# A planner that draws moved ranks stretch by stretch instead of for the whole order

## The chip, the cores and the metric

The kernel runs on one core of a Trainium2 chip. The time is that of one launch on the device in microseconds; it is the median of several runs. A profile of one further execution gives the busy time of each engine: TensorE (PE, with its weight loads as PEld), VectorE (DVE), ScalarE (ACT), GpSimd (POOL), and SyncE (SP), which issues the DMA transfers.

## The reference

One decoder layer over x of 32 sequences x 256 tokens x 256 features, all in float32. Three blocks follow each other, each on a layer norm of x and each added to x:

```python
x = x + self_attention(layernorm(x))   # gated slot attention, 4 heads, 64 slots
x = x + cross_attention(layernorm(x))  # 16 heads of 16, over 77 context rows, masked
x = x + experts(layernorm(x))          # 8 experts of rank 64, two of them weighted per token
```

The self attention projects to q, k (4 x 32), v (4 x 64), slot scores s (4 x 64) and a gate g. q, k and v go through a causal convolution of four taps and a SiLU, q and k through a rotation. Then come two causal linear attentions: q against k with the slot weights as values (`ok`), a softmax over the slots, and that against the slots with v as values (`ov`); in both, the weights are exp(s) over their running sum. A norm per head, the gate and an output projection end it. The cross attention is a plain softmax attention. The experts' hidden part is silu(u) * v for all eight experts, weighted by a softmax over the two largest router logits, and multiplied by the output weights.

## The kernel before

Everything works on one sequence at a time (the experts on two, 512 tokens; the last two sequences singly). The kernel's Python holds a planner, and the order in which instructions are issued to the engines is the planner's. Every engine then runs its own instructions in that order, and semaphores make one wait for the data or the buffer of another.

**Threads.** The work of a sequence is written as generators: `self_attention(n)`, `cross_attention(n)`, `experts(n, count)` and the parts that they start (`queries_keys`, `value`, `slot_weights`, `output_gate`, `weigh`, `context`, `weights`, `chunk`, `spread_weights`). At each step a generator yields what it wants: an engine and a time in ns, a list of alternatives, a buffer (`Take`), or an event. `ATTENTIONS` = 5 chains of self attentions, `CROSSINGS` = 3 chains of cross attentions and 2 chains of experts run at the same time; a further chain, `loads`, issues the loads of weights and of x on SyncE's queue.

**The clock of the plan.** `Flow.run` is a list scheduler over the planner's own cost figures. It takes, again and again, the step that can begin first, and among those that could begin at the same time the one of the lowest rank, since `threads` is sorted by rank:

```python
key = begin, whole, not thread[7]
if best is None or key < best[0]:
    best = key, wish, thread
```

Where a step offers alternatives, the one that ends first is taken. So `copy` goes to ScalarE or VectorE, `combine` (L647) to VectorE or GpSimd, `product` to VectorE or to ScalarE and GpSimd, and a convolution tap (L824) to VectorE or to ScalarE and GpSimd (L828, L831), as each engine is free in the plan. A changed order therefore also changes how much work each engine gets. PSUM is four single banks and two double ones, given out by `bank`; buffers in SBUF come in fixed numbers (`shapes`).

**Ranks.** `Flow.rank` gives a stage's start plus the sequence number plus a moved amount:

```python
return stage + n + self.moved.get((stage, n), 0.0)
```

with stages 0.0 (self attention), -1.0 (cross attention) and 3.0 (experts). A small move can put one sequence's steps behind or ahead of another's where both could begin.

**The search for moves.** `best_order` runs the whole plan on stand-ins (`Sketch`) 70 times. Each time it takes the best moves so far, redraws 20 of the 96 keys from a normal distribution with deviation 0.3, and keeps the result if the planned end is not later. The plan with the kept moves then emits the instructions.

**Names on TensorE.** In the order of a sequence's life: hT_ps (transposed layer norm, L680), s_ps, g_ps (L725), pr_ps (q, k and v, L716), ET_ps, v_ps (transposes, L880 for v), cp_ps<-qk, ok_ps<-cp (L739, L782), ok_ps and WT_ps (transposes), cp_ps<-WT, ov_ps (L739, L782), o_ps, oT_ps (transposes), wo_ps. Cross attention: K_ps, V_ps (L1127), hT_ps, Q_ps, sc_ps (L1183), eT_ps (L1241), av_ps (L1260), pj_ps. Experts: hT_ps, lgT_ps (L1304), lg_ps (L1312), wt_ps (L1362), u_ps and ev_ps (L716), eo_ps (L1461, and L1484 with wB_ps for the last two). cp_ps, ok_ps<-cp, ov_ps, sc_ps, av_ps and lgT_ps use only some rows or columns of the array and are issued in packed groups. On VectorE the heavy steps of self attention are the taps (L824), the causal masks (L758, L768), the running sums and reciprocals (L912, L918), and the statistics of the layer norm (L690, L691).

Of the kernel before, what the change touches and what calls it, by code (L numbers as in the profile page):

```python
# [43 lines left out]
PE, DVE, ACT, POOL, SP = "PE", "DVE", "ACT", "POOL", "SP"  # L44
# [6 lines left out]
RANK_SELF, RANK_CROSS, RANK_EXPERTS = 0.0, -1.0, 3.0  # L51
# [39 lines left out]

ORDERS, MOVED, BY = 70, 20, 0.3


class Sketch:


    def __init__(self, shape=(1,)):  # L100
        self.shape = tuple(shape)
# [53 lines left out]
class Flow:  # L155
# [6 lines left out]

    def __init__(self, slots, moved=None):
        self.moved = moved or {}
        self.slots = {tag: [(0.0, i) for i in range(n)] for tag, n in slots.items()}


        self.parts = WHOLE
        self.banks = {"bank": [0.0] * slots["bank"], "bank2": [0.0] * slots["bank2"]}
        self.free = defaultdict(float)  # L170

        self.port = 0.0
        self.busy = defaultdict(float)
        self.threads = []
        self.finish = 0.0
        self.count = 0

        self.changed = False

    def start(self, rank, part):  # L180
        self.count += 1
        thread = [rank, self.count, self.finish, part, None, None, 0.0, 0]
        thread[4] = next(part)
        self.threads.append(thread)
        self.threads.sort(key=lambda t: t[:2])
        self.changed = True

    def rank(self, stage, n):
        return stage + n + self.moved.get((stage, n), 0.0)

    def event(self):
# [86 lines left out]
    def run(self):  # L278
        while True:
            self.settle()  # L280
            if not self.threads:
                return
            best = None
            for thread in self.threads:
                wish = thread[4]
                if isinstance(wish, list):

                    _, begin, wish = min(self.end(thread, w) for w in wish)
                elif isinstance(wish, tuple):
                    begin = self.begin(thread, wish[0])  # L290
                else:
                    continue
                whole = False
                if wish[0] == PE:
                    _, _, tag, parts = wish
                    whole = parts is WHOLE
                    if tag:
                        got = self.bank(tag)
                        if not got:
                            continue  # L300
                        begin = max(begin, got[0] + HOP[PE])
# [5 lines that stand above are left out]
            if not best:  # L307
                raise Stuck
            (begin, _, _), wish, thread = best
            if wish[0] == PE and wish[3] != self.parts:  # L310
                begin = max(begin, self.free[PE] + SWITCH)
            engine, ns = REAL[wish[0]], wish[1]
            self.free[engine] = begin + ns
            if wish[0] in (BOTH, PAIR):
                self.port = begin + ns
            self.busy[engine] += ns
            thread[2] = begin + ns + TAIL.get(engine, 0.0)
            thread[5], thread[6] = engine, begin + ns
            if engine == SP:
                landing = Event()  # L320
                landing.time = begin + ns + LANDING
                self.resume(thread, landing)
            elif engine == PE:
                _, _, tag, self.parts = wish
                got = None
                if tag:
                    _, kind, slot = self.bank(tag, hold=True)
                    slots = slot if tag == "quad" else [slot]
                    got = [Buffer(self, kind, i, 1) for i in slots]
                    for buf in got:  # L330
                        buf.owner = thread
                    thread[7] += len(got)
                    got = got if tag == "quad" else got[0]
                self.resume(thread, got)
            else:
                self.resume(thread, wish[:2])


def best_order(plan, slots, sequences):


    rng = random.Random(0)
    keys = [
        (stage, n)
        for stage in (RANK_SELF, RANK_CROSS, RANK_EXPERTS) for n in range(sequences)
    ]
    best, kept = None, {}
    for _ in range(ORDERS):
        moved = dict(kept)
        if best is not None:  # L350
            moved.update({key: rng.gauss(0, BY) for key in rng.sample(keys, MOVED)})
        flow = Flow(slots, moved)
        try:
            plan(flow)
        except Stuck:
            continue
        if best is None or flow.finish <= best:
            best, kept = flow.finish, moved
    return kept


@with_exitstack
def decoder_layer(
# [28 lines left out]
    B, T, D = x.shape  # L392
# [29 lines left out]
    slots = {tag: s[0] for tag, s in shapes.items() if isinstance(s, tuple)}  # L422

    def lay_out(flow, nc, const, work, small, dram, psum):
# [363 lines left out]
        def self_attention(n):  # L788
# [58 lines left out]
            def queries_keys():  # L847
                yield have["k"]
                y2 = yield from conv_silu2(((wq_s, 0), (wk_s, 0)), (0, 1), "cv_qk")
                yield have["table"]  # L850
                y2.uses = 2

                yr = yield from take("rp")
                yield DVE, dve(512)
                nc.vector.stream_shuffle(yr.tile, y2.tile, SWAP)
                y2.drop()
                qk = yield from take("qk")
                yield from combine(qk.tile, y2.tile, cos.unsqueeze(1).to_broadcast(FEA), ALU.mult)
                y2.drop()
                yield from combine(yr.tile, yr.tile, sin.unsqueeze(1).to_broadcast(FEA), ALU.mult)  # L860
                yield from combine(qk.tile, qk.tile, yr.tile, ALU.add)
                yr.drop()
                got = yield from causal_products(qk.tile[:, 1:2, :], qk.tile[:, 0:1, :], HK)
                qk.drop()

                def weigh(c):
                    prods[c] = yield from causal_weights(got[c])
                    flow.set(ready[c])

                flow.start(rank, weigh(1))  # L870
                yield from weigh(0)
# [647 lines left out]
            flow.start(0, all_experts(i))  # L1519
        flow.run()  # L1520

    moved = best_order(lambda flow: lay_out(flow, *[Sketch()] * 6), slots, B)
    with tc.manual_schedule():
        lay_out(Flow(slots, moved), nc, const, work, small, dram, psum)

# [61 lines left out]
```

## Time and profile before

| what | us |
|---|---|
| median of 3 runs (1366.28 to 1367.6) | 1367.16 |
| the profiled execution | 1367.22 |
| its span, first to last instruction | 1365.4 |
| TensorE busy | 1316.1 (96%) |
| TensorE weight loads busy | 971.0 (71%) |
| VectorE busy | 1145.0 (84%) |
| ScalarE busy | 1040.9 (76%) |
| GpSimd busy | 634.2 (46%) |
| mean granted TensorE clock | 0.989 of full |

In the profile, the rows of digits cut the span into 40 slices of 34 us and give the busy share of each in tenths; PEclk is the clock that TensorE was granted. A row of a stretch gives the length, then the busy time of each engine with its number of instructions. A line of waits names who waited for whom, the total, how often, and the longest. Matmuls overlap, and the ends in the trace are modelled, so TensorE can be busy and yet not run at its best rate.

### The profile page before, as it was taken

To read this page: it belongs to the slowest core of one execution; us is meant where nothing else is said; L and a number is where in the kernel's file an instruction comes from. 1 tells how busy PE (TensorE), PEld (TensorE's weight loads), DVE (VectorE), ACT (ScalarE), POOL (GpSimd) and SP (SyncE) were. 2 spreads that over 40 slices of the span, in tenths; PEclk is the share of its full clock that TensorE was granted. 3 is DMA by queue.
4 is the path that set the end of the run, shared out by engine and by line. 5 is a ranking of instruction groups with operands and counts; after the bars stand their busy time and mean duration, and the time that the engine had idled before them with its cause. 6 is when DMAs were issued, how large, how long until landed. Compare 5 with 4: busy or idle time off the path is not lost.

```text
span 1365.4 us, 27161 instructions
## 1 busy us (share of the span) xinstructions
PE 1316.1 (96%) x9345; PEld 971.0 (71%) x9345; DVE 1145.0 (84%) x2268; ACT 1040.9 (76%) x4160; POOL 634.2 (46%) x805
## 2 busy tenths in 40 slices
PE   6989989999999999999999999999999999999898
PEld 5767766676868776876778678678676876757665
DVE  6999999777887976998789889998988799966554
ACT  4668898867878876886888678788888786886741
POOL 1546654524465724347543555554444355534220
PEclk9899999999999999999999999999999999999999
DMA  4600010122111122111121120111111211021110
GB/s 129 139 2 2 13 19 4 30 63 64 42 40 44 27 58 55 49 29 32 48 51 39 34 48 3 42 35 19 33 43 48 64 29 34 17 60 45 43 40 24
DMA packets 134202, 55.91 MB, mean 41 GB/s; under 512 B 106168, under 2 KB 125880, under 8 KB 134064
## 3 DMA queue, kind: packets, MB, share of 16 engines
q1 hardware_dynamic: 134064, 54.17, 16.7%
q8 instruction: 74, 1.21, 0.4%
q14 instruction: 64, 0.52, 0.1%
HBM read 42.37 MB, written 11.79 MB: 40 GB/s over the span
## 4 chain that ended last, share of the span: by engine, by line
PE 67%; DVE 25%; ACT 5%; POOL 2%; issue 1%; DMA 0%; ACTq 0%; DVEq 0%; POOLq 0%
PE ev_ps L716 8%; PE u_ps L716 8%; PE eo_ps L1461 6%; DVE y L824 5%; PE cp_ps L739 4%; PE eT_ps L1241 3%; PE av_ps L1260 3%; DVE RzT L918 3%; PE pj_ps L725 3%; PE pr_ps L716 3%; PE wo_ps L725 3%; PE sc_ps L1183 3%; PE ov_ps L782 3%; PE Q_ps L716 3%; PE hT_ps L680 2%; PE s_ps L725 2%
## 5 line engine op out<-in xcount | busy, mean ns | idle before, releaser
L1211 ACT ACTIVATE s<-s,s_mx 128x77 f32<-128x77 f32 x1024 | 359.0, 356 | 38.3 <-DVE s_mx L1206 38.0
L1211 ACT ACTIVATION_READ_ACCUMULATOR s<-s,s_mx 128x1 f32 x1024 | 201.5, 197 | 0.0
L824 DVE SCALAR_TENSOR_TENSOR y<-pr_ps,conv,y 128x254 f32<-128x254 f32 (+2 forms) x368 | 149.1, 469 | 4.7 <-ACT y L811 4.5
L671 POOL TENSOR_TENSOR rs_r<-rs_r,mhalf 128x2 f32<-128x2 f32 (+1 forms) x128 | 128.1, 1001 | 10.7
L702 ACT ACTIVATE ln_h<-xs,ln_off,rs_r 128x256 f32<-128x256 f32 x192 | 110.8, 597 | 22.8 <-POOL ln_off L696 21.3
L1191 DVE TENSOR_TENSOR s<-sc_ps,cap 128x616 f32<-128x616 f32 x128 | 98.7, 784 | 26.9 <-PE sc_ps L1183 26.7
L716 PE MATMUL ev_ps<-hT_e,ev_s 128*128 128x512 f32 (+1 forms) x272 | 120.8, 572 | 0.1
L716 PE MATMUL u_ps<-hT_e,eu_s 128*128 128x512 f32 (+1 forms) x272 | 119.1, 571 | 0.4 <-DVE y L824 0.4
L647 POOL TENSOR_TENSOR esT<-e_th,wB 128x512 f32<-128x512 f32 x55 | 73.3, 1335 | 93.0 <-DVE e_th L1415 74.1
L1461 PE MATMUL eo_ps<-eo_s,esT 128*128 128x256 f32 x480 | 115.6, 384 | 0.0
L670 POOL TENSOR_SCALAR rs_r<-ln_mv 128x2 f32<-128x2 f32 x96 | 25.6, 267 | 185.6 <-DVE ln_mv L691 167.2
L918 DVE RECIPROCAL RzT<-RzT 128x256 f32<-128x256 f32 x64 | 110.7, 1733 | 0.0
L1461 PEld LDWEIGHTS eo_ps<-eo_s,esT 128*128 128x128 f32 x480 | 87.4, 190 | 14.0 <-issue 3.3
L968 ACT ACTIVATE ok<-ok,ok_mx 128x64 f32<-128x64 f32 x256 | 87.4, 344 | 8.9 <-DVE ok_mx L965 8.9
L1241 PE MATMUL eT_ps<-cst,s 128*128 128x128 f32 x640 | 88.3, 278 | 3.8 <-POOL s L647 1.7
L1206 DVE TENSOR_REDUCE s_mx<-s 128x16 f32<-128x1232 f32 x64 | 91.1, 1423 | 0.8
L1241 PEld LDWEIGHTS eT_ps<-cst,s 128*128 128x128 f32 x640 | 75.6, 143 | 18.4 <-issue 7.0
L647 POOL TENSOR_TENSOR s<-s,s_rs 128x1232 f32<-128x1232 f32 x28 | 63.2, 2257 | 53.7 <-DVE s_rs L1217 53.6
L690 DVE BATCH_NORM_STATS2 ln_st<-xs 128x6 f32<-128x256 f32 x192 | 78.4, 408 | 8.0 <-DMA xs<-in_x_dram 7.6
L716 PEld LDWEIGHTS u_ps<-hT_e,eu_s 128*128 128x128 f32 x272 | 49.3, 190 | 42.3 <-issue 39.0
L758 DVE TENSOR_TENSOR cp<-cp_ps,cst 128x768 f32<-128x768 f32 x78 | 72.5, 939 | 6.1 <-PE cp_ps L739 6.1
L638 ACT ACTIVATE eT<-eT_ps 128x1024 f32<-128x1024 f32 x64 | 65.6, 1026 | 14.6 <-PE eT_ps L1241 14.4
(167 smaller groups left out, 3432.5 us busy)
## 6 DMA issues: line engine op xcount, KB each, us to landing
wB<-wd SPq DMA_DIRECT2D x60, 256.0 KB
Vb<-spread_v SPq DMA_DIRECT2D x32, 320.0 KB
xs<-in_x_dram SPq DMA_DIRECT2D x32, 256.0 KB
out_dram<-xs SPq DMA_DIRECT2D x32, 256.0 KB
cx<-in_ctx_dram SPq DMA_DIRECT2D x32, 77.0 KB
spread_v<-V SPq DMA_DIRECT2D x32, 77.0 KB
spread_v<-zeros SPq DMA_DIRECT2D x2, 309.0 KB
mk<-in_mask_Bx1xSxS_bk_dram SPq DMA_DIRECT2D x32, 19.2 KB
```

The lines of the kernel that those rows point to most:

```text
L647: engines[engine].tensor_tensor(to, a, b, op)
L671: nc.gpsimd.tensor_tensor(r, r, mhalf[:, :n], ALU.pow)
L702: nc.scalar.activation(h.tile[:, t, :], xt[:, t, :], AF.Identity, bias=off[:, t : t + 1], scale=rstd[:, t : t + 1],)
L716: nc.tensor.matmul(ps, lhsT=w[:, d], rhs=hT[:, d, :], start=(d == 0), stop=(d == ND - 1))
L725: nc.tensor.matmul(pv[:, t, :], lhsT=hT[:, d, ts(t, P)], rhs=w[:, d, :], start=(d == 0), stop=(d == n - 1),)
L824: nc.vector.scalar_tensor_tensor(y.tile[:, u, s:], now, by, y.tile[:, u, s:], ALU.mult, ALU.add)
L918: nc.vector.reciprocal(Rz.tile[:, c, :], Rz.tile[:, c, :])
L1191: nc.vector.tensor_tensor(sv[:, 2 * a : 2 * a + 2], got[a].tile[:, :, : ND * QR * S2].rearrange("p r (h k) -> p r h k", k=S2), cap.tile[:, ...
L1206: nc.vector.tensor_reduce(mx.rearrange("p (q h) -> p q h", h=QH), sv, AX.X, ALU.max, negate=True)
L1211: nc.scalar.activation(sv[:, h // QH, h % QH, :], sv[:, h // QH, h % QH, :], AF.Exp, bias=mx[:, h : h + 1], accum_out=sm[:, h : h + 1],)
L1241: nc.tensor.transpose(flat[:, ts(NTT * i + t, P)], s[t].tile[:, column : column + P], ident)
L1461: nc.tensor.matmul(halves(ps.tile)[:, t, :], lhsT=sT.tile[:, d, ts(NTT * b + t, P)], rhs=eo_s[:, d, :], start=(d == 0), stop=(d == NEC - 1),)
```

## The change

`best_order` no longer judges whole plans. It goes through the plan in stretches of 200 us of planned time. For each, it plans from the beginning to 50 us past the stretch with the moves kept so far, and then 16 times with new moves for about half of those keys whose rank had not been asked for before the stretch began. It keeps the moves with which TensorE has had most work planned by that point. When a plan reaches its end, the planned end decides. `Flow` notes when each rank is asked for (`asked`) and stops planning at `until`. The planner's costs, the generators and the instructions themselves are as before.

```diff
--- before.py
+++ after.py
@@ -91,7 +91,8 @@
 
 
 
-ORDERS, MOVED, BY = 70, 20, 0.3
+
+DRAWS, STRETCH, BEYOND, MOVED, BY = 16, 200000.0, 50000.0, 0.5, 0.3
 
 
 class Sketch:
@@ -162,6 +163,8 @@
 
     def __init__(self, slots, moved=None):
         self.moved = moved or {}
+
+        self.asked, self.until = {}, math.inf
         self.slots = {tag: [(0.0, i) for i in range(n)] for tag, n in slots.items()}
 
 
@@ -186,6 +189,7 @@
         self.changed = True
 
     def rank(self, stage, n):
+        self.asked[stage, n] = self.finish
         return stage + n + self.moved.get((stage, n), 0.0)
 
     def event(self):
@@ -307,6 +311,8 @@
             if not best:
                 raise Stuck
             (begin, _, _), wish, thread = best
+            if begin > self.until:
+                return
             if wish[0] == PE and wish[3] != self.parts:
                 begin = max(begin, self.free[PE] + SWITCH)
             engine, ns = REAL[wish[0]], wish[1]
@@ -336,27 +342,39 @@
                 self.resume(thread, wish[:2])
 
 
-def best_order(plan, slots, sequences):
+def best_order(plan, slots):
 
 
     rng = random.Random(0)
-    keys = [
-        (stage, n)
-        for stage in (RANK_SELF, RANK_CROSS, RANK_EXPERTS) for n in range(sequences)
-    ]
-    best, kept = None, {}
-    for _ in range(ORDERS):
-        moved = dict(kept)
-        if best is not None:
-            moved.update({key: rng.gauss(0, BY) for key in rng.sample(keys, MOVED)})
+
+    def drawn(moved, until):
         flow = Flow(slots, moved)
+        flow.until = until
         try:
             plan(flow)
         except Stuck:
-            continue
-        if best is None or flow.finish <= best:
-            best, kept = flow.finish, moved
-    return kept
+            return -math.inf, flow
+        if flow.threads:
+            return flow.busy[PE] - max(0.0, flow.free[PE] - until), flow
+
+        return 1e9 - flow.finish, flow
+
+    kept, begin = {}, 0.0
+    while True:
+        until = begin + STRETCH + BEYOND
+        best, flow = drawn(kept, until)
+        free = [key for key, at in flow.asked.items() if at >= begin]
+        choice = kept
+        for _ in range(DRAWS):
+            moved = dict(kept)
+            moved.update({key: rng.gauss(0, BY) for key in free if rng.random() < MOVED})
+            done, other = drawn(moved, until)
+            if done > best:
+                best, choice = done, moved
+        kept = choice
+        begin += STRETCH
+        if best > 0.5e9:
+            return kept
 
 
 @with_exitstack
@@ -1519,7 +1537,7 @@
             flow.start(0, all_experts(i))
         flow.run()
 
-    moved = best_order(lambda flow: lay_out(flow, *[Sketch()] * 6), slots, B)
+    moved = best_order(lambda flow: lay_out(flow, *[Sketch()] * 6), slots)
     with tc.manual_schedule():
         lay_out(Flow(slots, moved), nc, const, work, small, dram, psum)
```

## The prediction

> **What bounds the kernel now.** I read the busy slices first, then the busy time of each engine by stretch, then the waits of TensorE and the chain that ended last. The slices:
>
> ```profile
> PE   6989989999999999999999999999999999999898
> DVE  6999999777887976998789889998988799966554
> PEclk9899999999999999999999999999999999999999
> ```
>
> TensorE is full nearly everywhere; what it loses lies in the first eight slices and the last three. VectorE is full in slices 1 to 6 and never again for so long. In microseconds (columns after the stretch: its length, busy time of PE, PEld, DVE, ACT and POOL with counts, granted clock, DMA share, GB/s):
>
> ```profile
> 0.00:24.00 24.00, 16.53 (x70) 13.77 (x71) 11.22 (x31) 9.81 (x19) 5.56 (x14) 1.00 0.56 166
> 24.00:40.00 16.00, 9.31 (x50) 6.81 (x49) 14.65 (x30) 7.21 (x16) 4.99 (x6) 0.71 0.48 106
> 40.00:102.00 62.00, 54.62 (x387) 42.88 (x386) 59.90 (x112) 40.66 (x141) 32.34 (x36) 0.94 0.25 56
> 102.00:249.00 147.00, 136.58 (x1111) 106.69 (x1111) 141.66 (x276) 129.84 (x555) 87.36 (x105) 1.00 0.06 11
> 249.00:1195.00 946.00, 941.00 (x6791) 694.48 (x6790) 818.79 (x1601) 753.33 (x3034) 461.41 (x582) 1.00 0.17 40
> 1195.00:1330.00 135.00, 128.79 (x823) 85.07 (x816) 83.32 (x175) 94.22 (x387) 41.06 (x59) 0.96 0.20 47
> 1330.00:1365.40 35.40, 29.25 (x130) 21.29 (x128) 15.48 (x48) 5.78 (x15) 1.44 (x4) 1.00 0.07 23
> ```
>
> Of 49.3 us in which TensorE is idle, 32.0 lie before 249 us (249 less 217.0 busy), 5.0 in the 946 us that follow, 12.4 after 1195. Before 249 us VectorE is idle for 21.6 us, 12.8 of them in the first 24, while the first loads land. So there are two regimes: VectorE sets the pace until about 249 us, TensorE afterwards. The largest waits at the start, and the chain where the first regime ends (start, length):
>
> ```profile
> PE v_ps L880 <- DVE cv_v L840: 6.7, 1, 6.7
> 248.63 2.13 PE ov_ps L782 x16
> ```
>
> A total of busy time hides a second loss, since a busy TensorE can be slow. So I added up its work from start-to-start times of back-to-back matmuls in the timeline: 429 ns for 512 columns, 216 for 256, 109 for a 128x128 transpose, 0.74 us for a group of 16 on 32 rows, 1.51 and 1.45 us for those on 64 rows or columns, 1.87 us for the 32 of av_ps, 93 ns to enter a packed group. That makes 1273 us. The other 92 of the span are loss, and the trace says where: when 200 us of this work are done it is 248.6 us (48.6 lost); from there to the end 43.8 are lost.
>
> **The change, part by part.** No computation changes. What the draws keep is seen in the order in which the built kernels' instructions stand.
>
> *TensorE's work.* The same matmuls; 413 changes of packing against 412. At 0.1 to 0.3 us each: +0.2 us, nothing.
>
> *Which engine does the optional steps.* L647's combinations on VectorE fall from 68 to 52 of 316, by mean durations of 0.7 us (1.6 for s): about -13 us. Six more L824 steps (0.4) and ten more copies of 0.7: about +9. VectorE is 4 us lighter in all, GpSimd has 16 combinations of 1.3 us or so more. GpSimd is busy 46% and TensorE waits on it briefly: off the path after 249 us. Here a rule speaks against the change. The Trainium skill, "SBUF — State Buffer", section "Who interferes with whom", says that a VectorE instruction with two SBUF inputs and a GpSimd instruction that reads SBUF exclude each other for the whole instruction. By the rule alone each added combination may hold VectorE for its 1.3 us: up to 21 us. By the row, L840 (two SBUF inputs) takes 668 to 678 ns in the median and 931 at worst among 64, so nearly all wait for nothing: 16 x 0.05 is under 1 us. I take 0 and keep +3 for the range.
>
> *The first 250 us.* Up to 28 us little moves. Then the old order goes to v_ps, which waits 6.7 us. The new one puts 18.2 us of projections and transposes, mostly of sequences 2 to 4, ahead of the first cp_ps (by the durations above: three hT, ET and v_ps of 0.44 each, three s, two g, two wq/wk pairs and two wv of 1.73, one V of 0.43). Their inputs come sooner too: on SyncE's queue the loads of xq, xp, bp and of x for sequences 3 and 4 stood behind the store of V (31.1 us) and now stand ahead of it. Those 1.15 MB need 4.6 us at the 253 GB/s of 41 to 51 us; they land by about 25 us, and VectorE reads them at about 32. The store of V and the read of Vb come later, but av_ps wants them after 100 us: nothing. The scaling of wo_s by gn moves up in VectorE's queue to about 23 us; wo_s has landed by 14.5 us (SyncE reuses its queue slot then): nothing.
>
> Filling that wait is not yet a gain, because VectorE still has its work to do. So I asked at every matmul that reads what VectorE wrote: how much VectorE work (mean durations, in the built order) stands ahead of that write, and how much TensorE work ahead of the matmul? The excess is a wait that TensorE can't escape. Before, it rises to 17 at 67 us of TensorE work and peaks at 28.7 at 200 (ov_ps: 228.7 of VectorE). Adding VectorE's 21.6 us idle gives 250.3 against 248.6 in the chain, so the sum holds within 1.7 us. After, it is 0.3 at 43, 14 at 68, and peaks at 17.9 at 207. The new order does 7 us more TensorE work (a wo_ps, a u_ps pair among it) by that point and has 4 us less on VectorE. With VectorE's idle time unchanged the first regime sheds 28.7 - 17.9 = **10.8 us**. Bounds: if VectorE idles for only the unavoidable 12.8 plus 3 us, 16.6; if the early pile of projections leaves it waiting for ACT or GpSimd for 11 us more, 0. I take 10.8.
>
> *The middle.* I compared links (matmul, steps on other engines, matmul) with less than 0.5 us of spare TensorE work between: 27 before, 25 after, from 260 to 1120 us of work. Nothing; +-5 us, which is the idle time there now.
>
> *The end.* The last 45 rows are alike. Earlier TensorE ran out of cover (its waits from 1283.5 to 1290.3 us: total, times, longest):
>
> ```profile
> PE hT_ps L680 <- ACT ln_h L702: 0.9, 2, 0.5
> PE lgT_ps L1304 <- ACT hT_e L638: 0.6, 1, 0.6
> PE lg_ps L1312 <- ACT lgT L638: 0.6, 1, 0.6
> ```
>
> The new order puts four eo_ps (1.7 us) ahead of that lgT_ps and four ahead of lg_ps: -1.2 us. The clock adds to this (stretches of TensorE alone: length, busy, granted clock):
>
> ```profile
> 92.20:99.10 6.90, 6.09 (x30) 0.51 0.02 5
> 242.50:249.30 6.80, 4.36 (x38) 1.00 0.01 4
> 249.30:252.70 3.40, 3.40 (x24) 0.50 0.26 28
> 1198.20:1201.60 3.40, 3.40 (x17) 0.50 0.08 11
> 1290.30:1297.20 6.90, 5.14 (x24) 0.51 0.00 0
> ```
>
> The Trainium skill, "TensorE: Matmul & The Clock Gate", Part 1, has the clock halve after an idle window of about 3.4 us. By that only the 6.7 us wait would qualify, and the end would gain 1.2. The trace differs: from 242.5 to 249.3 TensorE was busy for 4.4 of 6.8 us, with no single wait over 2.1, and still ran at half clock for 3.4. So short waits in a row cost clock too: at the end (3.40 + 5.14) / 2 = 4.3 us. I take half, 2.1, as two such places may become one; the end sheds **3.3** (0 to 8).
>
> Sum: 1365.4 - 10.8 - 3.3 = 1351.3 us of span; the profiled execution took 1367.22, 1.8 more than its span, as the median (1367.16) does. **Predicted: 1353 us.**
>
> **Rivals.** *Given back:* the first sequence's cp_ps comes at about 46 us instead of 38, attentions finish later, VectorE idles 11 us more; the result is 1364 to 1369. For it: VectorE's work at the first wo_ps is 78 us, 74 before. Against: the excess is lower at 15 of the 17 15-us steps of TensorE work up to 255.
>
> *A stretch runs dry (slower):* after the early rush no attention starts between 419 and 533 us of TensorE work, then five start by 624. If those five lack crossings and experts for cover, as the first ten did, they cost what those did: (48.6 - 7) / 10 = 4.2 us each, 21 in all: 1374. It decides from 17 us on, four of five uncovered. Against: the old order, too, pauses from 698 to 754 and then starts four by 798, denser, and TensorE was idle for 5 us in all from 249 to 1195.
>
> *More than counted:* VectorE idles only 16 us and both half-clock places at the end vanish: -16.6 - 5.5, 1345.
>
> *No effect:* that every draw loses and the order stays; excluded, it differs from TensorE's 30th row on.
>
> **How the numbers follow.** 0.66 for the forecast (1347 to 1362), 0.12 for more, 0.11 for given back, 0.11 for slower. About 0.2%, 2.7 us, is what a measurement can tell: faster 0.78, same 0.11, slower 0.11. The range, 1343 to 1366, leaves out the slower rival, the top of the one given back and the far end of the larger gain.
>
> **What would show it.** TensorE idle before 249 us falls from 32 to about 20, v_ps's 6.7 us wait goes, and ov_ps or eT_ps near 207 us of work stands at about 245. The waits of lgT_ps and lg_ps near 1290 us go. From 249 to 1195 the loss stays. Wrong: VectorE idle over 30 us in the first 249, or new waits above 5 us together in the middle.

## The result

The changed kernel takes **1373.29 us** (median of 4 runs, 1369.79 to 1374.38), the kernel before 1367.0 on the same chip: a ratio of 1.0040, with a 95% interval of 1.0028 to 1.0051. A second set of runs of the same two gave 1373.36 and a ratio of 1.0051 (1.0036 to 1.0066). So it is slower by 6 us; 14 us less were predicted. The profiled execution took 1374.38, its span 1372.6.

The slices of the changed kernel:

```profile
PE   7869998999999999999999999999999999899998
DVE  6988999886998798786998879997788998967553
PEclk9989999999999999999999999999999999999999
```

The first slice (to 34 us) is fuller than before, a 7 where a 6 stood; the next two (to 103 us) are an 8 and a 6 where a 9 and an 8 stood. The same by stretches (length, then busy time of PE, PEld, DVE, ACT and POOL with counts, granted clock, DMA share, GB/s):

```profile
0.00:24.00 24.00, 16.44 (x67) 13.58 (x68) 10.71 (x30) 9.65 (x18) 5.20 (x14) 1.00 0.74 220
24.00:40.00 16.00, 14.30 (x72) 11.72 (x70) 15.83 (x39) 11.34 (x25) 7.20 (x15) 1.00 0.72 134
40.00:102.00 62.00, 48.03 (x325) 36.05 (x327) 56.73 (x87) 34.07 (x127) 35.96 (x29) 0.86 0.10 28
102.00:249.00 147.00, 138.80 (x1125) 109.26 (x1125) 138.84 (x266) 128.94 (x547) 89.02 (x109) 0.99 0.05 9
249.00:1195.00 946.00, 934.46 (x6728) 687.57 (x6729) 816.47 (x1613) 737.59 (x2978) 454.83 (x582) 1.00 0.17 40
1195.00:1330.00 135.00, 129.91 (x883) 86.28 (x882) 89.98 (x188) 102.91 (x436) 48.93 (x68) 0.99 0.19 45
1330.00:1372.60 42.60, 36.38 (x157) 27.17 (x155) 16.86 (x50) 6.16 (x16) 1.44 (x4) 0.93 0.07 25
```

From 24 to 40 us TensorE does 14.3 us instead of 9.3: the wait of 6.7 us for v_ps is gone. From 40 to 102 it gives that back (48.0 instead of 54.6, at a clock of 0.86 instead of 0.94). Before 249 us TensorE is idle for 31.4 us, 32.0 before the change. VectorE idles 26.9 us there, not 21.6. What TensorE waits for most between 40 and 102 us (total, times, longest):

```profile
PE ok_ps L800 <- DVE cp L786: 3.4, 1, 3.4
PE WT_ps L698 <- POOL ok L665: 2.7, 2, 1.9
PE ok_ps L698 <- DVE okT L672: 2.7, 2, 1.8
```

These are steps of the first attentions' chains. In the new order the projections stand ahead of them, and once these are done TensorE waits for one step of the chains after another (lines of the changed kernel are 18 higher than those of before).

To see where time is lost I take the **lateness**: the time at which a given amount of TensorE's work is done, less that work, both counted as in the prediction.

| TensorE work done, us | 40 | 60 | 80 | 200 | 240 | 1100 | 1140 | end of span |
|---|---|---|---|---|---|---|---|---|
| before, us late | 24.3 | 25.4 | 33.6 | 49.5 | 51.5 | 68.5 | 73.6 | 92.4 |
| after | 16.9 | 35.9 | 39.0 | 52.6 | 55.4 | 76.8 | 83.1 | 99.6 |

After 40 us of work the new order is 7.4 ahead; 20 us of work later it is 10.5 behind. At 240 it is 3.9 behind, at 1100 it is 8.3 behind, at 1140 9.5, and the last part regains 2.3: 7.2 in all, the difference of the two spans.

### The profile page after: what moved, and what is told of

It is laid out like the page before. It is cut to its first block, busy times and chain, and to the rows that moved or that the text cites. A ratio compares the mean times of both kernels' runs of the same rounds, so it can differ in the third digit from the quotient of the medians.

```text
span 1372.6 us, 27142 instructions
## 1 busy us (share of the span) xinstructions
PE 1318.3 (96%) x9345; PEld 971.6 (71%) x9345; DVE 1145.4 (83%) x2268; ACT 1030.7 (75%) x4144; POOL 642.6 (47%) x818
## 3 DMA queue, kind: packets, MB, share of 16 engines
q8 instruction: 74, 1.21, 0.4%
## 5 line engine op out<-in xcount | busy, mean ns | idle before, releaser
L842 DVE SCALAR_TENSOR_TENSOR y<-pr_ps,conv,y 128x253 f32<-128x253 f32 (+2 forms) x374 | 151.0, 470 | 23.4 <-ACT y L829 22.5
L734 PE MATMUL u_ps<-hT_e,eu_s 128*128 128x512 f32 (+1 forms) x272 | 122.7, 581 | 0.5 <-DVE y L842 0.5
L1209 DVE TENSOR_TENSOR s<-sc_ps,cap 128x616 f32<-128x616 f32 x128 | 98.9, 784 | 24.3 <-PE sc_ps L1201 24.1
L1479 PEld LDWEIGHTS eo_ps<-eo_s,esT 128*128 128x128 f32 x480 | 87.7, 190 | 13.9 <-issue 2.3
L986 ACT ACTIVATE ok<-ok,ok_mx 128x64 f32<-128x64 f32 x256 | 87.0, 343 | 10.6 <-DVE ok_mx L983 10.6
L665 POOL TENSOR_TENSOR s<-s,s_rs 128x1232 f32<-128x1232 f32 x30 | 67.4, 2249 | 43.4 <-DVE s_rs L1235 40.3
L734 PEld LDWEIGHTS u_ps<-hT_e,eu_s 128*128 128x128 f32 x272 | 49.5, 194 | 40.6 <-issue 35.7
L734 PEld LDWEIGHTS ev_ps<-hT_e,ev_s 128*128 128x128 f32 x272 | 48.8, 190 | 39.7 <-issue 36.0
```

Source lines behind the costliest of these rows:

```text
L665: engines[engine].tensor_tensor(to, a, b, op)
L734: nc.tensor.matmul(ps, lhsT=w[:, d], rhs=hT[:, d, :], start=(d == 0), stop=(d == ND - 1))
L842: nc.vector.scalar_tensor_tensor(y.tile[:, u, s:], now, by, y.tile[:, u, s:], ALU.mult, ALU.add)
L986: nc.scalar.activation(ok[:, i, :], ok[:, i, :], AF.Exp, bias=mx[:, i : i + 1], accum_out=sm[:, i : i + 1],)
L1209: nc.vector.tensor_tensor(sv[:, 2 * a : 2 * a + 2], got[a].tile[:, :, : ND * QR * S2].rearrange("p r (h k) -> p r h k", k=S2), cap.tile[:, ...
L1479: nc.tensor.matmul(halves(ps.tile)[:, t, :], lhsT=sT.tile[:, d, ts(NTT * b + t, P)], rhs=eo_s[:, d, :], start=(d == 0), stop=(d == NEC - 1),)
```

## Experiments

Three theories. **Plan:** the chip follows the planner's plan, and the new search found a plan that is no better. The planner's own cost figures give its planned end for any moves: 1363.8 us for the kernel before, 1367.0 for the one after. **Port:** VectorE instructions are held up by GpSimd's combinations, which the prediction took as nothing. **Pile:** the early projections leave the attention chains uncovered at 57 to 96 us.

### No moves, the first stretches, another seed

```diff
 e1: moved = {}
 e2: the search returns after its first stretch (begin >= 200000.0), e3 after three (600000.0)
 e4, on the kernel before:
-    rng = random.Random(0)
+    rng = random.Random(9)
```

> The changed kernel with no rank moved at all (moved = {}). The planner's own planned end for this order is 1406.6 us (1363.8 for the kernel before, 1367.0 for the kernel after). Theory PLAN (the chip follows the plan, so the change lost because its search found a worse plan): planned end plus 3 to 6, as before (+3.2) and after (+6.3) stand to their plans: 1410 to 1413. Theory CHIP (what the plan doesn't know, VectorE slowed beside GpSimd and VectorE's idle time in the first 100 us, decides between orders): no tie to the planned end; 1370 to 1400.

> The changed kernel's search ended after the first stretch: the moved ranks kept for 0 to 200 us only, nothing moved later. Planned end 1374.1. The order of the first 250 us is the one of the kernel after. Theory PLAN: 1377 to 1380, that is 4 to 7 slower than after; the planner has the loss after 400 us. Theory CHIP: the loss against before lies in the first 100 us, which this kernel shares with after, so the state at 250 us (some 4 us later than before) is the same in both, and the rest decides for 1368 to 1385.

> The changed kernel's search ended after three stretches (0 to 600 us). Judged by TensorE's planned work 50 us past each stretch, the second and third choice gained 1.6 and 4.9 us over leaving the ranks alone; yet the planned end went from 1374.1 to 1394.4 and 1414.9. Theory PLAN: 1418 to 1421, slower than the first stretch alone by about 40, all of it after 1000 us of the span. Rival GREEDY HOLDS (TensorE work gained by 650 us stays gained on the chip, the planned tail is an artefact of the plan): as fast as the first stretch alone or up to 6 us faster, 1371 to 1379.

> The kernel before (70 draws over the whole plan, judged by the planned end) with its random numbers begun from 9 instead of 0. Planned end 1355.8, 8.0 less than the kernel before; the plans' TensorE work is the same up to 600 us and differs after 800. Theory PLAN: 8 us less than before, 1359 to 1361. Theory CHIP: the first 250 us are as before, so nothing is gained from VectorE or GpSimd there; 1365 to 1370.

Measured: e1 1414.3, e2 1385.6, e3 1418.9, e4 1359.2 us (ratio to before 0.9941, 0.9927 to 0.9956). Seed 9 has the best plan of twelve seeds of the search before. The chip puts these orders as the planner does. Theory PLAN holds for such differences, with an error of its own: e1 came 1 and e2 6 us above what was expected of them.

e3 against e2 is a direct test of the new judge. The second and third stretch's choices were kept because they gave 1.6 and 4.9 us more TensorE work, 50 us past the stretch. On the chip e3 is 10.6 us less late than e2 at 1000 us of work (69.5 against 80.1; 3.1 of this stand at 40 us already), and it ends 33 us later. From 1080 us of the span on, e3:

```profile
1080.00:1417.00 337.00, 293.20 (x1905) 201.54 (x1903) 219.32 (x441) 198.15 (x820) 113.97 (x139) 0.94 0.12 30
```

The waits of TensorE in this stretch:

```profile
PE hT_ps L698 <- ACT ln_h L720: 9.2, 6, 4.0
PE wt_ps L1380 <- DVE tp_wt L1377: 3.6, 1, 3.6
PE eT_ps L1259 <- DVE s L665: 3.5, 2, 1.9
PE ev_ps L734 <- DVE e_th L1424: 3.4, 1, 3.4
PE eo_ps L1479 <- POOL esT L665: 3.1, 3, 1.8
```

No engine is full here, TensorE waits for one link after another, and its clock is 0.94. So what is won by 650 us isn't kept: the rival GREEDY HOLDS falls. That the work done early is the very work that would have covered these waits is how I read it; no run takes it apart.

### Two more searches

```diff
 e7, on the kernel after:
-    rng = random.Random(0)
+    rng = random.Random(1)
 e8, on the kernel after, with random.Random(7): each draw planned to the end, and judged by that
-            done, other = drawn(moved, until)
+            done, other = drawn(moved, math.inf)
```

> The kernel after with its random numbers begun from 1 instead of 0. Planned end 1376.4 (after: 1367.0; the mean of twelve such seeds is 1382, that of twelve seeds of the search before 1369). Theory PLAN, corrected by the runs so far (chip above plan by 3.2 to 11.5, median 5): 1380 to 1385, slower than after, so that the order that the change happened to get was a good draw of its search. Rival LUCK (the chip doesn't tell such plans apart): 1368 to 1376, as after.

> The kernel after, where each stretch's draws are judged by the planned end of the whole plan instead of TensorE's work 50 us past the stretch; random numbers begun from 7. Planned end 1363.3; eight seeds of this judge have a mean of 1370, against 1382 for the judge of the change and 1369 for the search before. So the plans say that the judge costs the time and not that ranks are drawn stretch by stretch. Theory JUDGE: the chip follows, 1366 to 1370, some 3 to 7 less than after. Rival STRETCHES (drawing stretch by stretch costs it, whatever judges): 1372 or more.

Measured: e7 1387.3, e8 1372.6 us. (The mean planned end of the twelve searches of the change is 1380, not the 1382 of the expectations.) e7 is 14 slower than after, 2 above its range, so the change's seed 0 was a good draw of its search and LUCK falls. e8 missed: planned 3.7 below after (the best plan of eight seeds), it ran as after, just inside the range of its rival STRETCHES. One seed can't tell the judge from the drawing by stretches. That the judge is what costs is the planner's figure alone (mean planned ends 1380 with TensorE's work as judge, 1370 with the planned end, 1369 for the search over whole orders); e3 shows what it can do, not its average price.

### GpSimd's combinations made narrow

In e5 (from before) and e6 (from after), every combination or product of the helpers `combine` and `product` that works in place on GpSimd is done on 2 columns and followed by a power of 2 columns, so that GpSimd is busy about as long and hardly reads. g2 (from after) and g3 (from before) do it only for what the plan places before 250 us.

```diff
+        def thin(to, b, op, times=1):
+            to, b = [v[(slice(None),) + (0,) * (len(v.shape) - 2) + (slice(0, 2),)] for v in (to, b)]
+            nc.gpsimd.tensor_tensor(to, to, b, op)
+            for _ in range(times):
+                nc.gpsimd.tensor_tensor(to, ones[:, :2], to, ALU.pow)
...
-            engines[engine].tensor_tensor(to, a, b, op)
+            if engine == PAIR and to is a:      # g2, g3: and flow.finish < 250000.0
+                thin(to, b, op, 2 if columns > 1000 else 1)
+            else:
+                engines[engine].tensor_tensor(to, a, b, op)
```

> The kernel before, each GpSimd combination or product that works in place (rotation terms, rotated sum, ok, o, s, xs plus bias, okT, WT) replaced by the same operation on 2 columns and a power of 2 columns (1.0 us for the latter in the rows of rs_r), so that GpSimd is busy for about as long, at the same place in every queue, but hardly reads SBUF. Left out: the values of all but 2 columns of these combinations. Theory PORT (a VectorE instruction that meets a GpSimd combination waits until it ends): VectorE's time above its medians, 2.8 us before 250 us, falls to about 1; the kernel gains 1 to 3: 1364 to 1366. Theory ORDER (the order alone costs the time): within 1 us of before plus or minus what a shorter s step gives, 1365 to 1367.

> The kernel after, with the same replacement (left out: the values of all but 2 columns of GpSimd's in-place combinations and products). Theory PORT: VectorE's time above its medians before 250 us falls from 10.8 to about 3, and as VectorE sets the pace there, 200 us of TensorE work are done about 6 us sooner, 46 to 47 us late instead of 52.6; the kernel takes 1365 to 1368, and its gap to the kernel before with the same replacement is 0 to 3 instead of 6. Theory ORDER (the pile of projections and its waits at 57 to 96 us, which the planner's own plan holds too, cost the time): the excess may vanish, but the stall at 57 to 96 us and the gap of 6 stay: 1370 to 1373.

> The kernel after, unchanged, for a second profiled execution. Theory START (the load of the first sequences makes the start differ by 3 us from run to run): 40 us of TensorE work come either 14 or 17 late, and the lateness at 240 us moves with it: 52.3 or 55.4. Rival FIXED: 17 and 55.4 again. Time as before, 1370 to 1374.

> The kernel after, GpSimd's in-place combinations and products made 2 columns wide plus a power of 2 columns, only those that the plan places before 250 us (left out: the values of all but 2 columns of these). Theory PORT: VectorE's time above its medians before 250 us falls from 10.8 to 4.5, the lateness at 240 us to 46 to 49, and what is won there is kept to the end: 1367 to 1370. Theory REFILL (VectorE freed of the hold-ups idles more, as TensorE and GpSimd then come too late for it): the lateness at 240 us falls by 3 or less against an execution with the same start, VectorE idles 3 more, 1370 to 1373.

> The kernel before with the same edit (left out: the same values). VectorE's time above its medians before 250 us is only 2.8 there. Theory PORT: 1 to 2 us less, 1364.5 to 1366, so that the gap between the two narrow kernels is 1 to 5 instead of 6.3. Theory REFILL: as in the run with all of them narrow, 240 us of work 48.6 late instead of 51.5, 1363 to 1365, and the gap stays 6 or more.

What was suspected, in the trace of the kernel after (timeline: start, length, instruction):

```profile
88.98 1.27 POOL L665 TENSOR_TENSOR qk<-qk,rp 128x512 f32<-128x512 f32 x1
89.03 1.76 DVE L930 TENSOR_TENSOR_SCAN RzT<-cst,ET 128x256 f32<-128x256 f32 x1
```

The running sum takes 1.76 us where it takes 0.68 alone: 1.08 longer, for an overlap of 1.21 with GpSimd's rotated sum. The same group in the first 250 us (busy us, mean ns), after:

```profile
L930 DVE TENSOR_TENSOR_SCAN RzT<-cst,ET 128x256 f32<-128x256 f32 x20 | 18.4, 923 | 0.0
```

Before:

```profile
L912 DVE TENSOR_TENSOR_SCAN RzT<-cst,ET 128x256 f32<-128x256 f32 x20 | 13.5, 677 | 0.0
```

With the narrow combinations (g2):

```profile
L944 DVE TENSOR_TENSOR_SCAN RzT<-cst,ET 128x256 f32<-128x256 f32 x20 | 15.3, 767 | 0.0
```

Over all of VectorE's groups, the time above the group's median is 10.8 us before 250 us in the kernel after, 2.8 in the one before, 4.3 in g2 and 1.3 in g3. (What is left in g2 stands beside steps of GpSimd that the edit leaves as they are, mostly the first rotation product, qk from cv_qk, and the clamp of E.)

Times: e5 1360.1 (4 us below both of its ranges), e6 1366.1; g1 1373.4, g2 1368.8 (12 runs, 1365.3 to 1371.4), g3 1364.6. Narrow before 250 us alone brings 4.5 us from after to g2 (1373.3 to 1368.8) and 2.1 from before to g3 (1366.7 to 1364.6). The gap between the two orders shrinks from 6.6 to **4.2**: by the medians, the hold-ups of the first 250 us explain some 2.4 us of it. Three things keep this figure rough:

- Executions of one kernel differ by when the clock rises (last section), and the medians mix them. A count that leaves the start out: from 40 to 240 us of work g2 loses 34.4 us; after, g1, e2 and e3, which have the same order of TensorE there, lose 38 to 39. So the narrow combinations save some 4 us in this order. In that of before they save 2.6 (g3), and 1.5 us of the gap is left to the hold-ups.
- GpSimd is busy for less time, too: from 102 to 249 us 82.6 us in g2 instead of 89.0, and 76.9 in g3 instead of 87.4. That a part of the gain comes from GpSimd being done earlier stands untested.
- Narrow everywhere brings 7.2 and 6.6, and the gap of 5.9 stays, as Theory ORDER of e6 said, though the time is PORT's. With 2.4 us explained it should have come down here as well.

g2's time is in Theory PORT's range and g3's in both. REFILL asked for a comparison with an execution of the same start. g1 isn't one: 40 us of work are done 16.4 us late in it, 14.7 in g2 and 13.7 in e3. VectorE idles 27.5 us in g2, 24.2 in e3 and 26.2 in g1. So by the traces the truth lies between the two theories: VectorE's time above its medians falls by 6.5 us, some 4 of them reach TensorE, and VectorE idles away the rest.

The stall stays: e6 loses 19.7 us between 40 and 60 us of work. For g2, the two stretches that lost time after the change:

```profile
40.00:102.00 62.00, 46.61 (x355) 35.12 (x353) 57.17 (x93) 35.40 (x136) 32.90 (x46) 0.92 0.10 27
102.00:249.00 147.00, 140.90 (x1147) 111.51 (x1145) 137.50 (x267) 129.76 (x554) 82.63 (x146) 1.00 0.06 11
```

The second gains 2.1 us of TensorE work; the first doesn't, its waits are the pile's. g1 repeats after: 16.4 late at 40 us of work, 54.5 at 240. Theory START isn't seen between these two executions, but it isn't excluded either: of the eight timed runs of this kernel one took 1369.8 us at a mean clock of 0.992, the other seven 1371.6 to 1374.4 at 0.988 to 0.990.

### One tie

The first stretch kept eleven moves. Nine of them, dropped one at a time, leave the planned end and TensorE's planned work as they are. One of the other two settles the start: crossing of sequence 1 (rank -1 + 1) ties with the attention of sequence 0 (rank 0). The change's draw puts the crossing ahead, the old search's draw the attention. (By the `key` shown with the planner, rank decides only among steps that are also alike in packing and in whether their thread holds PSUM.)

```diff
 f3: moved = {(RANK_CROSS, 1): -0.1}
 f4: moved = {(RANK_SELF, 0): -0.1}
```

> One moved rank alone: crossing of sequence 1 at -0.1, so that it goes ahead of the attention of sequence 0, with which it ties unmoved. This alone makes the plan's start that of the kernel after (TensorE's planned work agrees at every mark to 150 us); nothing is moved later. Planned end 1380.5. What is read is the start: theory PORT PLUS PILE (the start of after has on the chip what the plan doesn't hold): by 240 us of TensorE work some 55 late, VectorE 10 above its medians before 250 us, no wait of v_ps near 6.7 us, a stall of 18 us between 40 and 60 us of work. Whole time 1384 to 1388.

> The other way of the same tie: attention of sequence 0 at -0.1, nothing else moved. The plan's start is that of the kernel before. Planned end 1395.5. What is read is the start: some 51.5 late by 240 us of TensorE work, VectorE 3 above its medians before 250 us, v_ps waiting 6.7 us, 1 us lost between 40 and 60 us of work. Whole time 1398 to 1402. Rival CHANCE (the differences in the first 250 us are from elsewhere in the order or from run to run): both starts alike within 1.5 us at 240 us of work.

Measured: f3 1386.6, f4 1403.0 us (2 runs each; f4 is 1 above its range). From 40 to 60 us of work f3 loses 18.8 us and f4 1.0, as after and before do (19.0, 1.1). VectorE's time above its medians before 250 us is 8.0 and 2.7. f4 has the old wait:

```profile
PE v_ps L898 <- DVE cv_v L858: 6.7, 1, 6.7
```

f3 hasn't. So this one tie settles the wait and the stall, and the rival CHANCE falls. It doesn't settle everything up to 240 us of work. There f3 is 56.2 late and f4 51.5, near after (55.4) and before (51.5); but TensorE has the order of before in f4 to 607 us of work, and that of after in f3 only to 115. From there f3 runs another order, whose plan has 3.4 us less TensorE work by 250 us than the plan of after, so that f3 comes out as late as after is partly luck. The later part is decided elsewhere: f3 starts worse than f4 and ends 16 us sooner.

### A longer search over whole orders

```diff
 on the kernel before; f2: 160 draws. f1: 620 draws, and random.Random(11)
-ORDERS, MOVED, BY = 70, 20, 0.3
+ORDERS, MOVED, BY = 160, 20, 0.3
```

> The kernel before with 620 draws instead of 70 and random numbers begun from 11. Planned end 1352.1, the lowest of twelve long searches; its start is neither that of before nor that of after. Theory PLAN alone: planned end plus 3 to 6: 1355 to 1358, faster than both kernels and than seed 9 (1359). Theory PLAN plus what the first 250 us add on the chip (0 for the start of before, 3 for that of after, up to 8 for others in these runs): up to 1363.

> The kernel before with 160 draws instead of 70, nothing else changed. The last draw that it keeps is number 155 and brings the planned end from 1363.8 to 1355.7; the plan of the first 250 us is that of before. Theory PLAN: 1359 (1358 to 1361), as the seed 9 order with 1355.8 planned.

Measured: f2 **1358.9** us, a ratio to before of 0.9947 (0.9933 to 0.9962), f1 1360.0. Both beat before and after. f2 is in its range; f1 is 2 above that of Theory PLAN alone and inside the wider one. f1's plan is 3.6 better than f2's and the chip doesn't show it. Its start isn't f2's: it is 1.4 us later at 240 us of work, and 3.5 at 1000.

Planned end and measured median of the twelve orders that compute everything:

| | f2 | e4 | f1 | e8 | before | after | e2 | e7 | f3 | f4 | e1 | e3 |
|---|---|---|---|---|---|---|---|---|---|---|---|---|
| planned, us | 1355.7 | 1355.8 | 1352.1 | 1363.3 | 1363.8 | 1367.0 | 1374.1 | 1376.4 | 1380.5 | 1395.5 | 1406.6 | 1414.9 |
| measured | 1358.9 | 1359.2 | 1360.0 | 1372.6 | 1366.7 | 1373.3 | 1385.6 | 1387.3 | 1386.6 | 1403.0 | 1414.3 | 1418.9 |

The chip stands 2.9 to 11.5 above the plan, 6.7 in the mean. All pairs that the plan puts over 5 us apart stand in its order; of the eight closer pairs four are reversed, two of them by less than 1 us.

## Why the prediction was wrong

**The first 250 us, -10.8 predicted: the step that failed.** The sum held: lateness at 200 us of work is the excess plus VectorE's idle time plus what its instructions take longer than in the kernel before. Two of its inputs didn't hold.

| | excess | VectorE idle before 249 us | longer than before | sum | measured |
|---|---|---|---|---|---|
| before | 28.7 | 21.6 | 0 | 50.3 | 49.5 |
| after | 17.9 | 26.9 | 8.0 | 52.8 | 52.6 |
| e3, the order of after, clock up sooner | 17.9 | 24.2 | 8.0 | 50.1 | 49.5 |
| g2, after narrow early | 17.9 | 27.5 | 1.5 | 46.9 | 46.3 |
| g3, before narrow early | 28.7 | 22.2 | -1.5 | 49.4 | 48.4 |

- "With VectorE's idle time unchanged (21.6 us before 249)": it was 26.9. This is half of the rival *given back*, which said 11 more. VectorE idles 3.2 us more than before from 40 to 102 us, mostly for WT_ps (2.6 us instead of 0.8), and 2.8 more from 102 to 249 us, in several waits of 1 to 2 us.
- "I take 0 and keep +3" for GpSimd's combinations: the term was **8.0** us. The Trainium skill's "SBUF — State Buffer", section "Who interferes with whom", was right, and the row that I set against it was read from an order in which few of these instructions happened to meet: 20 running sums at 677 ns before, 923 after. I had asked only what the 16 added combinations cost. What changed is which VectorE instruction each old one meets. The planner keeps such pairs apart in its plan: the running sums are steps of the class `BOTH`, the combinations on GpSimd of the class `PAIR`, and a step of either begins only when the last one of both is done (`port` in `Flow.begin` and `Flow.run`). So they meet only where the chip's times run off the plan's, and how far they do in a new order can't be read from the old one.

5.3 + 8.0 = 13.3 is more than the 10.8 that the excess sheds. The narrow runs put the second part's own share of the gap at the end at about 2.4 us by the medians, because before gained too.

Not all of this is the order's doing. TensorE has the order of after to 649 us of work in e3, too, and e3 is 3.1 us ahead of after at 240 us of work (52.3 late against 55.4), only 0.8 behind before:

```profile
0.00:249.00 249.00, 217.38 (x1609) 170.98 (x1610) 224.84 (x423) 185.47 (x722) 139.96 (x167) 0.97 0.18 43
```

Its clock rises earlier (last section), which the order doesn't decide. That the 10.8 us don't come holds for e3 as well.

**VectorE 4 us lighter:** its busy time is 1145.4 against 1145.0. Over the whole run its instructions take 38.7 us above their medians, 35.5 before: most of the 4 us went there.

**The middle, 0 within 5:** +4.4 by lateness (from 3.9 behind at 240 to 8.3 at 1100), inside the bound but not nothing. TensorE is idle for 11.5 us from 249 to 1195 us, 5.0 before: more than the 5 us of new waits in the middle that the prediction named as a sign of being wrong. They are many and short; the two largest:

```profile
PE cp_ps L757 <- POOL qk L665: 1.8, 3, 0.8
PE cp_ps L757 <- DVE WT L672: 1.4, 3, 0.5
```

The plan has this loss as well: TensorE's planned work, after less before, is +0.8 us at 250 us, -1.1 at 400, -6.5 at 800, -7.0 at 1200. (It has the stall, too: +8.3 at 60 us, -1.4 at 80.) Counting links with thin cover (25 against 27) did not see it, and which links cost it stays open. The rival of a *stretch that runs dry* did not come: from 520 to 640 us of work after loses 5.5 us and before 3.3, not 21 more.

**The end, -3.3:** the waits of lgT_ps and lg_ps near 1290 us are gone as foreseen, and from 1140 us of work on after regains 2.3. But between 1100 and 1140 it loses 6.3 (before 5.1), and from 1195 us to the end the waits for tp_wt, 2.1 us before, have grown to:

```profile
PE wt_ps L1380 <- DVE tp_wt L1377: 6.0, 3, 2.8
```

Of the 2.1 us counted for the clock, the rows give about 1: from 1195 us to the end the kernel before lost 5.4 us of full clock (135 us at 0.96), the one after 4.3 (135 at 0.99, 42.6 at 0.93). Net, the end brings -1.1.

**What was left out:** the planner's own planned end of the new order, 3.2 us worse. By the pairs above, 3 us of plan don't settle the sign; but no order of the table stands below its plan, and 1353 is 14 us below that of after.

## What to carry over

An order is worth what it leaves for the end: judging a piece of a schedule by the busy time shortly after it can buy a few microseconds and sell thirty, as e3 did. When work is reordered, keep neither the idle time nor the instruction durations of the pacing engine as constants: ask which instructions now run at the same time, and take the duration of one that met its rival, not the median. Where a planner decides, compare its own planned ends first, and trust only differences larger than those that measured pairs have reversed. And before a few microseconds are put down to a cause, compare executions whose clock rose at the same point.

## What the runs showed of the hardware

- A VectorE instruction with two inputs in SBUF that begins while GpSimd combines two SBUF tiles is lengthened by the overlap less 0.13 us: running sums by 0.67, 1.00 and 1.08 us for overlaps of 0.81, 1.14 and 1.21, cv_v by 0.61, 0.84 and 0.92 for 0.74, 0.98 and 1.06. GpSimd's 128 powers on few columns, 999 ns each in the kernel after, held up no VectorE instruction by more than 0.06 us.
- The clock can fall or not on the same waits. In the kernel after, its repeat and e2, TensorE ran at 0.72 of the clock from 40 to 46 us; after:

```profile
40.00:46.00 6.00, 5.32 (x19) 4.23 (x20) 6.00 (x11) 3.26 (x7) 2.75 (x2) 0.72 0.99 281
```

  and e3, with the same start:

```profile
40.00:46.00 6.00, 5.82 (x29) 5.15 (x30) 6.00 (x8) 3.79 (x9) 2.88 (x2) 1.00 0.70 221
```

  From 24 to 42 us TensorE's listed waits are the same in both (s_ps 1.2 us, hT_ps 1.1). What differs is when the clock first rises, which the traces show by the spacing of the first matmuls of 256 columns: it drops from 427 to 216 ns at 15.0 us in after and at 12.0 in e3. The later changes of the clock stand at whole multiples of 3.41 us from that point: in after it falls 27.3 us later and rises again 3.4 us after that; in e3 it first falls 51.2 us later, for 10.2. The three executions with the loss at 40 to 46 us rose latest (g1 14.1, e2 14.7, after 15.0), the four without it earlier (e3 12.0, e6 12.5, f3 13.1, g2 13.9). Of the 3.2 us that e3 is ahead at 40 us of work (13.7 late against 16.9), 1.5 are there by 16 us, from the earlier rise, and 1.7 come from 42 to 46 us. The Trainium skill, "TensorE: Matmul & The Clock Gate", Part 1, calls the window in which activity is judged free-running and its effect variable between runs; these traces agree. What sets the point in a given run, they don't show. g2 has the same luck: 2.2 us of what it is ahead of after stood at 40 us of work already and aren't due to the narrow combinations.
